# A Flamingo gated block on one core: the first steps behind the branch put in another order, and two filler products fewer

## The chip, the cores and the metric

The kernel runs on one core of one Trainium2 chip. The metric is the device time of one execution in microseconds (us); the figure for the kernel before is the median of three runs, 656.4 us (655.87 to 658.57).

## The reference

The inputs are `x` (16 sequences of 224 tokens, 512 wide), a context for each sequence (750 rows, 384 wide) and a mask of the context rows; which rows count is data, read on the chip. Cut to what matters:

```python
# x: (16, 224, 512)   context: (16, 750, 384)   mask: (16, 750)
q = (layernorm(x) @ W_q);  k = context @ W_k;  v = context @ W_v      # 8 heads of 64
sim  = where(mask, q k^T * 64**-0.5, -FMAX)
attn = softmax(sim) v
x = x + tanh(g_xattn) * (attn @ W_o + b_o)

def bitlinear(x, w, b):                    # int8-like rows, ternary weights
    xq = act_quant(rmsnorm(x));  wq = weight_quant(w)   # scale of w: mean(|w|) over all of w
    return xq @ wq.T + b
h = gelu(bitlinear(layernorm(x), w1, b1))  # 512 -> 2048
x = x + tanh(g_ffn) * bitlinear(h, w2, b2) # 2048 -> 512
```

## The kernel before

**Before the branch.** `order_batches` counts the mask rows, ranks the 16 sequences by how many context rows they need, and fetches the rows of the first place ("slot" 0) by gathers on POOL (GpSimd): two gathers of 128 tokens of `x` (`fetch_x`, L975) and two of context rows (`fetch_keys`, L1055). All engines then read one number, `n_odd`, and branch (L436, L437): if every slot fits its fixed capacity, the compact path runs, otherwise a dense one. The compact path runs here.

**Behind the branch.** The work is cut into named steps, and `ORDER`, a list written out by hand, gives the order in which they are issued. Each engine executes its own instructions in that order, and waits on semaphores for the others. So a place in the list is a place in the queue of every engine that the step uses. `s` counts slots (sequences in order of length), `t` blocks of 128 tokens, `i` pairs of such blocks. The steps that the change and the following sections speak of:

- `tokens` (L267 to L343, DVE): the table of row numbers for all later gathers of `x`: five small copies into `where`, and one multiply-add into `token`.
- `stats.0.k`, `rstd.0.k`, `norm.0.k`, k = 0 and 1 (L1258 to L1272): layernorm of the first two blocks of `x`. Mean and variance on DVE (`bs_x`, `mv_x`, `rs_x`), the power -1/2 on POOL (`rs_x<-rs_x,mhalf`, L1267), the normalising itself on DVE, in place (`xoT<-xoT,mv_x,rs_x`).
- `x.i.k` (L975, POOL): a gather of 128 rows of `x` by the table `token`; `ctx.s.t` (L1055, POOL): a gather of context rows by `keys`. POOL issues both, one after the other.
- `ind.s` (L1080, L1082, DVE, six instructions), `pi.s` (L1091, PE, two tiny products), `keys.s` (L1105, DVE, two instructions): the row numbers of the context rows that slot `s` keeps. `ind` has one buffer, so `ind.s` may begin only when the products of the slot before have read it.
- `warm` (L2137, PE): products of a matrix of ones with itself into a tile that nobody reads.
- `xnp.t` and `xnT.t.s`: turning the normalised rows on PE, and the copy out of PSUM; `ctxp`, `ctxT`: the same for context rows; `qp`, `kp`, `vp`, `vr`: the projections on PE; `sim`, `max`, `exp`: scores and softmax.
- `w.0.c` (L1992, SP's DMA queue): eight loads of 512 KB, the raw `w1`. `ws.0.c` sums their absolute values (DVE, L2006, where the list says `:v`; ACT, L2009, where it says `:s`); `wt.0` (L2019, DVE) adds the eight sums, `wtp.0` (L2024, PE) adds them across partitions, and `sw.0` gives the scale, without which no weight can be rounded. The same follows later for `w2` (`ws.1.c`, `wt.1`, `wtp.1`).
- `stats.i.k` for i > 0 (L1292, L1293, DVE): the statistics of a gathered block.

The buffers of PSUM that `pi`, `kp`, `qp` and others use come from one pool of four, given out in the order of the list; a step waits until the last reader of its buffer is done.

The selection steps in short:

```python
st["ind"] = ind = pa.tile([TJ, 192], BF16, tag="ind", bufs=1)            # ind.s
nc.vector.tensor_scalar(ind[:, at], place, sh.upto[:, 0, b : b + 1], None, ALU.is_ge)
for n in range(1, NJ):
    nc.vector.scalar_tensor_tensor(ind[:, at], place, sh.upto[:, n, b : b + 1], ind[:, at], ALU.is_ge, ALU.add)
```

Of the kernel before, what the change touches and what calls it, by code (L numbers as in the profile page):

```python
# [26 lines left out]
CAPS = (188, 188, 184, 180, 176, 168, 156, 148, 128, 124, 116, 104, 92, 80, 64, 64)  # L27

ORDER = """
hold.0 load.wv tokens stats.0.0 stats.0.1 rstd.0.0 rstd.0.1 x.2.0 norm.0.0 norm.0.1 ind.1 warm xnp.0 xnp.1 xnT.0.0:s  # L30
xnT.1.0:s xnT.1.1:s gap mask.0 ctxp.0.2 ctxp.0.0 qp.0.0 pi.1 ctxT.0.0:s ctxT.0.2:s keys.1 w.0.0 w.0.1 w.0.2 w.0.3
w.0.5 w.0.7 w.0.4 w.0.6 x.2.1 ctx.1.0 kp.0.0 ind.2 pi.2 x.1.0 x.1.1 ind.3 ws.0.1:s keys.2 stats.2.1 ctx.2.0 tanh
ws.0.0:v x.3.0 kp.0.2 kT.0.0:s stats.2.0 qT.0.0:s kT.0.0.c:s stats.1.1 rstd.2 ws.0.3:s sim.0.1 ws.0.2:v sim.0.0
ctx.1.1 kT.0.2:s ws.0.5:s vp.0 max.0.0.0 max.0.0.1 max.0.0.3 kT.0.2.c:s stats.1.0 exp.0.0.0 exp.0.0.1 max.0.1.0 rstd.1
exp.0.0.3 vr.0 max.0.0.2 v.0:s max.0.1.3 exp.0.0.2 norm.1.0 ws.0.4:v qp.0.2 v_rest.0:s norm.1.1 ws.0.7:s rec.0.0
# [888 lines left out]
def compact_path(ctx, tc, sh, x, context, out, late_rows, stages):  # L924
# [29 lines left out]
    def gen(shape, dtype, name):  # L954
        return ps_gen.tile(shape, dtype, tag="gen", name=name)
# [45 lines left out]
    def step(*key):  # L1001
        def keep(run):
            name = ".".join(str(k) for k in key)
            assert name not in steps, name
            steps[name] = run
            return run

        return keep
# [940 lines left out]
    @step("where")  # L1949
    def run():  # L1950
        late["where"] = [
            nc.values_load(
                sh.token[p : p + 1, t // 7, t % 7 : t % 7 + 1],
                engines=[mybir.EngineType.SP],
                min_val=0,
                max_val=B * S - n,
            )
            for p, t, n in ((0, NTOK - 4, 64), (64, NTOK - 4, S), (32, NTOK - 2, S))
        ]
# [115 lines left out]
    ctx = stages[0]  # L2075
# [57 lines left out]
    @step("warm")  # L2133
    def run():
        spare = gen([P, P], F32, "warm")
        for k in range(8):
            nc.tensor.matmul(spare, lhsT=sh.ones, rhs=sh.ones, start=True, stop=True)  # L2137

    @step("tokens")
# [76 lines left out]
```

## Time and profile before

| What | us |
|---|---|
| median of 3 runs (lowest, highest) | 656.4 (655.87, 658.57) |
| time of the profiled execution | 658.56 |
| its span | 656.8 |
| PE busy in the span | 633.6 (96%) |
| DVE, ACT, POOL busy | 494.2, 434.7, 380.8 |
| first product of the compact path that is read (`xnp.0`) | at 14.15 |
| longest waits of PE after that: for `wt.0`, then for `wt.1` | 2.7 (to 37.50), 1.8 (to 71.75) |

Times in the text are microseconds from the start of the span. Of the profiled execution's 658.56 us, 1.8 us lie outside the span. That execution was 2.2 us slower than the median. PE stands for TensorE's products and PEld for its weight loads, DVE for VectorE, ACT for ScalarE, POOL for GpSimd, SP for the engine that issues the plain DMAs. A wait is put down to the engine or transfer that ended it.

### The profile page before, as it was taken

The page shows a single profiled execution, that of the slowest core. Times are in us where ns is not written, and L with a number is a line of the kernel's source. Part 1 is how long each engine was busy: PE and PEld are TensorE (multiplying, and loading weights), DVE is VectorE, ACT ScalarE, POOL GpSimd, SP SyncE. Part 2 cuts the span into 40 slices and gives each one's busy share as a digit, 9 for nine tenths or more (in the row PEclk, how much of TensorE's full clock was granted, in tenths as well). Part 3 has the DMA queues.
Part 4 walks back from the last instruction along what each step waited for, and adds up shares of the span by engine and source line. Part 5 has one row for each costly group of instructions (what it writes and reads, how often), then busy time and mean ns, then how long its engine had stood idle before and what let it go on. Part 6 is the DMA issues. An engine that isn't in the chain of part 4 may idle for free.

```text
span 656.8 us, 11053 instructions
## 1 busy us (share of the span) xinstructions
PE 633.6 (96%) x3706; PEld 411.8 (63%) x3706; DVE 494.2 (75%) x1325; ACT 434.7 (66%) x985; POOL 380.8 (58%) x531
## 2 busy tenths in 40 slices
PE   6989899999999999999999999999999999999995
PEld 5767757767566585675756668656666755654442
DVE  6798788776874787777878577886595865858994
ACT  2489786767676673596757467875496554859694
POOL 6444558664866447663757763753776364564741
PEclk9999999999999999999999999999999999999999
DMA  6959682116233053312235521513243041433222
GB/s 204 371 81 304 196 199 69 45 49 110 66 87 86 32 80 91 84 34 61 65 77 80 96 75 34 92 46 58 64 117 73 17 97 50 95 65 81 48 33 86
DMA packets 97346, 60.73 MB, mean 92 GB/s; under 512 B 85461, under 2 KB 85609, under 8 KB 97152
## 3 DMA queue, kind: packets, MB, share of 16 engines
q1 hardware_dynamic: 89232, 35.41, 25.8%
q0 software_dynamic: 8048, 24.53, 12.4%
q8 instruction: 31, 0.51, 0.3%
q14 instruction: 35, 0.29, 0.1%
HBM read 31.87 MB, written 7.34 MB: 60 GB/s over the span
## 4 chain that ended last, share of the span: by engine, by line
PE 84%; DVE 6%; DMA 5%; ACT 2%; issue 1%; POOL 1%; DVEq 0%; POOLq 0%
PE hp L1671 14%; PE fp L1908 14%; PE qp L1345 14%; PE op L1547 13%; PE kp L1180 5%; PE vp L1207 5%; PE sim L1378 5%; PE ptp L1448 3%; PE av L1488 3%; DMA raw<-w 2%; PE xnp L1323 2%; DMA raw<-in_L_ffn_w_dram 2%; PE vr L1224 1%; DMA x<-in_x_dram,token 1%; PE ctxp L1160 1%
## 5 line engine op out<-in xcount | busy, mean ns | idle before, releaser
L1426 POOL TENSOR_TENSOR p<-p,rec 112x752 f32<-112x752 f32 (+13 forms) x64 | 73.2, 1149 | 134.4 <-DVE rec L1421 101.6
L1409 ACT ACTIVATE p<-p,nm 112x188 f32<-112x188 f32 (+13 forms) x256 | 102.0, 401 | 26.8 <-DVE nm L1395 25.8
L1345 PE MATMUL qp<-xnT,wq_sb 128*128 128x224 f32 x512 | 103.2, 355 | 0.0
L1671 PE MATMUL hp<-w1T,xqT 128*128 128x512 fp8e4 x448 | 102.1, 379 | 1.1 <-DVE h L1682 0.7
L1908 PE MATMUL fp<-w2T,hqT 128*128 128x512 fp8e4 x448 | 100.9, 379 | 0.7 <-ACT hqT L1713 0.7
L1547 PE MATMUL op<-wo_sb,xoT 128*128 128x512 f32 x224 | 101.0, 596 | 0.0
L1345 PEld LDWEIGHTS qp<-xnT,wq_sb 128*128 128x128 f32 x512 | 95.4, 190 | 4.9 <-issue 2.9
L1682 DVE SCALAR_TENSOR_TENSOR h<-hp,c,b_bc 128x1024 f32<-128x1024 f32 x52 | 66.6, 1282 | 31.3 <-PE hp L1671 26.5
L1671 PEld LDWEIGHTS <-xqT 128*128 128x128 bf16 x448 | 43.5, 98 | 51.3 <-issue 3.4
L1908 PEld LDWEIGHTS <-hqT 128*128 128x128 bf16 x448 | 43.1, 98 | 49.9 <-issue 1.1
L1547 PEld LDWEIGHTS op<-wo_sb,xoT 128*128 128x128 f32 x224 | 41.0, 190 | 44.7 <-issue 43.5
L1395 DVE CUSTOM_DVE_ANT_0 p<-sim,mask 112x64 f32<-112x64 f32 (+12 forms) x224 | 54.9, 281 | 18.7 <-PE sim L1378 12.0
L1731 DVE TENSOR_REDUCE a<-h 128x1 f32<-128x2048 f32 x26 | 59.2, 2277 | 1.1 <-ACT h L1726 1.1
L1726 ACT ACTIVATE h<-h 128x2048 f32<-128x2048 f32 x26 | 49.7, 1913 | 11.6 <-DVE h L1682 11.4
L1180 PE MATMUL kp<-ctxT,wk_sb 128*128 128x188 f32 (+12 forms) x360 | 52.4, 295 | 0.9 <-ACT pT L1025 0.9
L1180 PEld LDWEIGHTS kp<-ctxT,wk_sb 128*128 128x128 f32 x360 | 49.2, 191 | 5.9 <-issue 3.3
L1025 ACT COPY pT<-ptp 128x448 f32<-128x448 f32 (+6 forms) x54 | 28.1, 528 | 32.1 <-PE ptp L1448 30.1
L1409 ACT ACTIVATION_READ_ACCUMULATOR p<-p,nm 112x1 f32 x256 | 48.7, 190 | 0.0
L1757 ACT ACTIVATE h<-h 128x2048 f32<-128x2048 f32 x25 | 47.8, 1911 | 1.0 <-DVE hq L1737 1.0
L1378 PE MATMUL sim<-kT,qT 64*112 64x188 f32 (+13 forms) x512 | 42.5, 296 | 0.9 <-ACT xoT L1025 0.6
L1646 POOL TENSOR_TENSOR y<-y,b_bc 128x512 f32<-128x512 f32 x28 | 36.1, 1295 | 12.1 <-DVE xoT L1023 9.4
L1207 PE MATMUL vp<-wv_sb,ctxT 128*128 128x512 f32 (+5 forms) x90 | 41.6, 598 | 0.0
(211 smaller groups left out, 1161.4 us busy)
## 6 DMA issues: line engine op xcount, KB each, us to landing
raw<-in_L_ffn_w_dram SPq DMA_DIRECT2D x16, 512.0 KB, 5.5
wq_sb<-in_L_xattn_W_q_dram SPq DMA_DIRECT2D x1, 1024.0 KB
b_bc<-in_L_ffn_b_dram SPq DMA_DIRECT2D x1, 1024.0 KB
wk_sb<-in_L_xattn_W_k_dram SPq DMA_DIRECT2D x1, 768.0 KB
wv_sb<-in_L_xattn_W_v_dram SPq DMA_DIRECT2D x1, 768.0 KB
wo_sb<-in_L_xattn_W_o_dram SPq DMA_DIRECT2D x1, 512.0 KB, 11.6
wo_sb<-in_L_xattn_W_o_dram SPq DMA_DIRECT2D x2, 256.0 KB
out_dram<-y SPq DMA_DIRECT2D x2, 256.0 KB
```

The costliest lines, as they stand in the source:

```text
L1180: nc.tensor.matmul(pk[:, p - p0, :], lhsT=sh.wk[:, c, p * P : (p + 1) * P], rhs=st["ctxT"][:, c, :n], start=(c == 0), stop=(c == NC - 1),)
L1207: nc.tensor.matmul(pv[:w], lhsT=st["ctxT"][:, c, :w], rhs=sh.wv[:, c, :], start=(c == 0), stop=(c == NC - 1))
L1345: nc.tensor.matmul(pq[:, i, :], lhsT=sh.wq[:, d, (p + i) * P : (p + i + 1) * P], rhs=st["xnT"][:, d, :], start=(d == 0), stop=(d == ND - 1),)
L1378: nc.tensor.matmul(sim[:, j, i, :cap], lhsT=st["qT"][j * DH : (j + 1) * DH, p, q * TQ : (q + 1) * TQ], rhs=keys["kT"][j * DH : (j + 1) * D ...
L1395: nc.vector.tensor_tensor_reduce(out=probs[:, h, :cap], in0=box["sim"][:, j, i, :cap], in1=keys["mask"][:, first + j * begin : first + j * ...
L1409: nc.scalar.activation(box["p"][:, h, :cap], box["p"][:, h, :cap], AF.Exp, bias=box["nm", h], scale=-1.0, accum_out=total[:TQ, h : h + 1],)
L1426: nc.gpsimd.tensor_tensor(probs[:, :, first : first + cap], probs[:, :, :cap], box["rec"][:TQ].unsqueeze(2).to_broadcast([TQ, 4, cap]), AL ...
L1547: nc.tensor.matmul(po, lhsT=xoT[:, d, at : at + P], rhs=sh.wo[:, d, :], start=(d == 0), stop=(d == ND - 1))
L1671: nc.tensor.matmul(ph[:, n, :], lhsT=f["xqT"][:, k * ND + d, :], rhs=w1T[:, d, at : at + NB], start=(d == 0), stop=(d == ND - 1),)
L1682: nc.vector.scalar_tensor_tensor(h[:, cols], f["hp", k, g].rearrange("t i n -> t (i n)"), f["c1", k], sh.b1[:, cols], ALU.mult, ALU.add,)
L1731: nc.vector.tensor_reduce(amax[:, part], f["h", k], AX.X, ALU.max, apply_absolute_value=True)
L1908: nc.tensor.matmul(po, lhsT=f["hqT", k][:, n, :], rhs=w2T[:, n, :], start=(n == 0), stop=(n == NF - 1))
```

## The change

Three edits. In `ORDER`, `tokens` goes from ahead of the statistics of the first two blocks to behind their normalising, and `x.2.0` stays behind it. In `ORDER` again, `ind.2` goes from behind `kp.0.0` to ahead of `keys.1`. In `warm`, six products are issued in place of eight. Everything from `pi.2` on stands as it did.

```diff
 ORDER = """
-hold.0 load.wv tokens stats.0.0 stats.0.1 rstd.0.0 rstd.0.1 x.2.0 norm.0.0 norm.0.1 ind.1 warm xnp.0 xnp.1 xnT.0.0:s
-xnT.1.0:s xnT.1.1:s gap mask.0 ctxp.0.2 ctxp.0.0 qp.0.0 pi.1 ctxT.0.0:s ctxT.0.2:s keys.1 w.0.0 w.0.1 w.0.2 w.0.3
-w.0.5 w.0.7 w.0.4 w.0.6 x.2.1 ctx.1.0 kp.0.0 ind.2 pi.2 x.1.0 x.1.1 ind.3 ws.0.1:s keys.2 stats.2.1 ctx.2.0 tanh
+hold.0 load.wv stats.0.0 stats.0.1 rstd.0.0 rstd.0.1 norm.0.0 norm.0.1 tokens x.2.0 ind.1 warm xnp.0 xnp.1 xnT.0.0:s
+xnT.1.0:s xnT.1.1:s gap mask.0 ctxp.0.2 ctxp.0.0 qp.0.0 pi.1 ctxT.0.0:s ctxT.0.2:s ind.2 keys.1 w.0.0 w.0.1 w.0.2
+w.0.3 w.0.5 w.0.7 w.0.4 w.0.6 x.2.1 ctx.1.0 kp.0.0 pi.2 x.1.0 x.1.1 ind.3 ws.0.1:s keys.2 stats.2.1 ctx.2.0 tanh
 ws.0.0:v x.3.0 kp.0.2 kT.0.0:s stats.2.0 qT.0.0:s kT.0.0.c:s stats.1.1 rstd.2 ws.0.3:s sim.0.1 ws.0.2:v sim.0.0
...
     @step("warm")
     def run():
         spare = gen([P, P], F32, "warm")
-        for k in range(8):
+        for k in range(6):
             nc.tensor.matmul(spare, lhsT=sh.ones, rhs=sh.ones, start=True, stop=True)
```

On DVE the order of instructions becomes: `bs_x`, `mv_x`, `rs_x` twice, both normalisings, the six of `tokens`, `ind.1`, the fills and masks that stood behind it, `ind.2`, `keys.1`, `ind.3`, `keys.2`. On POOL nothing changes place: the two powers, then `x.2.0`, `x.2.1`, `ctx.1.0`, `x.1.0`, `x.1.1`, `ctx.2.0`. On PE the order is the same, with four instructions fewer (an f32 product is two). ACT and SP are as before.

## The prediction

> **What bounds the kernel now.** I read the page's busy shares and its chain first.
>
> ```profile
> PE 633.6 (96%) x3706; PEld 411.8 (63%) x3706; DVE 494.2 (75%) x1325; ACT 434.7 (66%) x985; POOL 380.8 (58%) x531
> PE 84%; DVE 6%; DMA 5%; ACT 2%; issue 1%; POOL 1%; DVEq 0%; POOLq 0%
> ```
>
> PE is the bound, and between 100 and 600 us it hardly ever stands still (over 99.8% busy in those windows). The change leaves all of that work alone. What it can move is the time at which PE's unbroken run begins, so the chain in order of time is read next, over the first 38 us (start, length, what).
>
> ```profile
> 11.44 0.19 DVE token L343
> 11.63 0.61 DVE bs_x L1258
> ...
> 23.72 6.31 DMA x<-in_x_dram,token
> 30.05 0.70 DVE bs_x L1292
> ...
> 37.50 0.37 PE wtotp L2024 x2
> ```
>
> The table `tokens` stands in the chain ahead of the first statistics; the selection of slot 1 leads to POOL's gathers; the gather of `x.1.1` takes 6.31 us from issue to use and ends a wait of DVE, whose next instructions then run without a gap until `wt.0`. PE waits for that sum; this is its longest wait behind the branch (time, count, longest):
>
> ```profile
> PE wtotp L2024 <- DVE wtot L2019: 4.5, 2, 2.7
> DVE bs_x L1292 <- DMA x<-in_x_dram,token: 0.7, 1, 0.7
> DVE keys L1105 <- PE pi L1091: 2.4, 1, 2.4
> ```
>
> After 37.50 PE runs full until 60, and the rounding of the weights hangs on the same sum, through their transposes and the loads of `w2` to the second such wait at 71.75. So a shift of `stats.1.1` at 30.05 goes through to the end, one for one. That is the quantity to work out.
>
> **Edit one, statistics ahead of the table.** `tokens` occupies DVE from 10.36 to 11.63, 1.27 us. Without it the first statistics start at 10.36: their data came from a gather issued at 5.87, and the context gather issued at 9.38 released ACT at 12.49, 3.11 later, so I put the two blocks at 9.0 and 10.5 at the latest, both in time. `rs_x` is then ready at 11.4 in place of 12.63. But POOL stands ahead of the gain:
>
> ```profile
> 11.70 0.50 POOL L222 IOTA place_f<- 128x192 bf16 x2
> 12.15 0.10 POOL L337 MEMSET mhalf<- 128x2 f32 x1
> 12.79 0.59 POOL L1267 TENSOR_TENSOR rs_x<-rs_x,mhalf 128x1 f32<-128x1 f32 x1 [0.54 <-DVE rs_x L1262]
> 13.72 0.78 POOL L1267 TENSOR_TENSOR rs_x<-rs_x,mhalf 128x1 f32<-128x1 f32 x1 [0.35 <-DVE rs_x L1262]
> ```
>
> POOL issues gathers until 11.65 and fills `mhalf` until 12.25. The first power can come no earlier than 12.3: 0.5 gained of 1.27. The second follows at 12.9 and, at its slower 0.78, ends at 13.7 in place of 14.50; the second normalising ends 0.8 earlier. On PE `xnp.0` moves from 14.15 to 13.66 and `xnp.1` from 15.19 to 14.5, since its four products ahead (0.85) now set it: 0.7 for everything up to `qp.0.0` and `pi.1`. The instructions that move back: `tokens` now runs from about 14.3 to 15.6, and `ind.1`, the fills and masks end at 18.7 in place of 18.22. The 2.4 us in which DVE waited for `pi.1` hide that. On POOL `x.2.0` must now wait for `token` and goes from 14.68 to 15.7; only `x.2.1` and `ctx.1.0` queue behind it, and POOL was idle for 4.0 us ahead of `ctx.1.0`. The rows of `x.2.1` are wanted at 26.51; with 6.31 from an issue at 17.0 they land at 23.3. Cost: nothing, unless landing took over 9 us.
>
> **Edit two, `ind.2` ahead of `keys.1`.**
>
> ```profile
> 20.62 0.33 DVE L1105 TENSOR_SCALAR keys<-pi,first 128x1 int32<-128x1 f32 x2 [2.40 <-PE pi L1091]
> 20.88 0.25 DVE L1080 TENSOR_SCALAR ind<-place,upto 125x192 bf16<-125x192 bf16 x1
> 21.11 1.00 POOL L1055 DMA_INDIRECT ctx<-in_ctx_dram,keys  x1 [4.01 <-DVE keys L1105]
> 21.17 2.24 DVE L1082 SCALAR_TENSOR_TENSOR ind<-place,upto,ind 125x192 bf16<-125x192 bf16 x5
> ```
>
> `ind.2` takes 20.88 to 23.41, 2.53 us, and may not start before `pi.1` has read the buffer, so it inherits the wait of `keys.1`. `keys.1` then comes 2.53 later against `pi.1`. Queued behind its wait on POOL: `ctx.1.0`, `x.1.0` and `x.1.1`, all late by 2.53, 1.3 us apart. In return `pi.2`, `ind.3`, `keys.2` come some 0.3 earlier against `pi.1`, being spared the 0.33 of `keys.1` or part of it. `kp.0.2` takes the PSUM buffer of `pi.1` and now waits for `keys.1`; that ends about when it used to start (23.69 before, 3.2 us behind `pi.1` in both orders): nothing.
>
> **Edit three, six products.** Eight took 10.14 to 13.89, 0.47 us each. PE then waited 0.26 for the normalising. Two fewer end at 12.95, so `xnp.0` at 13.66 isn't blocked; eight would cost it 0.23. But these products also keep PE active, and its pace is seen to change (min/median/max ns of one turning product):
>
> ```profile
> L1323 PE MATMUL xnp<-ident,xoT x8: 397/421/477, 14.2 to 15.9; 128*128 128x128 f32 x8
> L1323 PE MATMUL xnp<-ident,x x8: 272/273/331, 38.3 to 41.3; 128*128 128x128 f32 x8
> ```
>
> The same product took 421 early and 272 late, 298 on average in `ctxp` from 16.10, though the clock column says 1.00 for both. PE comes to full pace near 16.1, after some 5.6 us of products. If the same sum is needed, full pace comes 0.3 later (0.94 less work, 0.5 earlier start, most of it in `ctxp`): I take +0.3. The bounds: nothing, or all of `qp.0.0` (3.22) at the early pace, another 2.9.
> [...]
>
> **The sum.** `pi.1` releases DVE at 20.62 - 0.7 + 0.3 = 20.2. `x.1.1` is issued at 23.72 - 0.4 + 2.53 = 25.85. DVE reaches `stats.1.1` at 29.35 - 0.4 - 0.2 = 28.75, so its landing decides. Rows: 6.31 while the weights load, 3.11 when little else does. The transfer share by window says which is nearer (us, PE, PEld, DVE, ACT, POOL busy, clock, DMA share, GB/s):
>
> ```profile
> 26.00:32.00 6.00, 6.00 (x37) 3.38 (x36) 5.19 (x12) 2.38 (x6) 4.13 (x6) 1.00 1.03 380
> 32.00:40.00 8.00, 5.27 (x39) 4.55 (x39) 7.46 (x30) 6.91 (x27) 4.78 (x7) 1.00 0.07 18
> ```
>
> The queues are full to about 32. The gathers' bytes only move later, so the weights clear a little sooner; I take 6.0. Landing 31.85 against 30.05: **+1.8 us**. DVE's wait there grows from 0.7 to about 3, PE's wait for `wt.0` from 2.7 to about 5. Against the profiled execution: 658.56 + 1.8 = 660.4. That execution lay 2.2 above the median; the same shift on the median gives 656.4 + 1.8 = **658.2**, which is 0.3% and inside the 0.5% (3.3 us) that a measurement of this kernel can tell from no change.
> [...]
>
> **The rivals.**
> *The gathers are not late where it counts.* If landing is set by the end of the weight loads and not by the issue, `x.1.1` lands 3.11 after its issue, at 28.96: 1.1 earlier than before, 655.3; the floor is DVE's own 28.75, -1.3. For it: the gathers no longer compete from 25 on. Against it: 380 GB/s until 32, and all eight loads are issued before 20.
> *PE's clock, slower by over 0.5%.* One mechanism: too little activity. All of `qp.0.0` at the early pace gives 2.6 more than my 0.3, so +4.4, 660.8; the growth of PE's wait for `wt.0` from 2.7 to 5 can do it a second time, as the products behind 37.5 would run at 421 in place of 272 (2.7 us of idle left them at 272). It decides from 1.5 us on top of my sum. Against it: half of what PE loses behind 37.5 comes back in its waits of 0.9 and 1.8 us before 71.75.
> *Edit one brings nothing* (POOL no earlier than 12.79): `pi.1` 0.7 later, +2.5, 658.9; within the forecast's range.
>
> **How the numbers follow.** Forecast with its variants, +0.2 to +3.2: 0.58, own range 656.6 to 659.6. Clock, over +3.3: 0.30, plus 0.02 for landings slower than 6.31. Gathers in time, -1.3 to 0, with the scatter of single runs (655.87 to 658.57) about it: 0.10, of which 0.04 over 0.5% faster. Slower 0.32, faster 0.04, the same 0.64. The range leaves out one in ten on each side: 655.4 from the second case, 661.2 from the clock at +4.4 with a little scatter.
>
> **What would show it.** Right: first power on POOL near 12.3, `keys.1` about 2.2 later than 20.62, DVE waiting 2 to 4 us for `x` at L1292, PE's wait for `wt.0` near 5, and no other stage changed in length. Wrong: no wait at L1292 (the landing), `pi.1` at 21 or later with `qp` products over 400 ns (the clock), or a shift at 37.5 that is gone by 72.

## The result and the profile after

The changed kernel takes 660.1 us (median of 10 runs, 658.41 to 660.95) against 656.3 us of the kernel before (10 runs beside it, 655.73 to 658.57). The ratio is 1.0047, 95% interval 1.0037 to 1.0058: slower by 3.1 us (2.4 to 3.8). The forecast was 658.2 with a range of 655.4 to 661.2; the time lies inside the range, between the forecast's own upper end (659.6) and the clock rival (660.8). Ratios here and below leave out single executions more than 1.5% above the fastest of their kernel (five in all, at 740 to 3708 us).

The page of the changed kernel, its busy shares and its chain:

```profile
PE 634.6 (97%) x3702; PEld 412.4 (63%) x3702; DVE 494.0 (75%) x1325; ACT 434.5 (66%) x985; POOL 379.7 (58%) x531
PE 87%; DVE 4%; DMA 3%; ACT 2%; issue 2%; POOL 1%; DVEq 0%; POOLq 0%; ACTq 0%
```

PE was busy for 1 us longer with four instructions fewer: some products ran more slowly (in the timelines the sixteen of `sim` near 40 take 2.94 in place of 1.58). The chain in order of time shows which (start, length, what):

```profile
12.45 0.60 POOL rs_x L1267
...
13.67 1.27 PE xnp L1323 x8
14.95 0.94 PE ctxp L1160 x6
15.89 3.23 PE qp L1345 x16
...
21.82 0.26 DVE keys L1105 x2
...
24.82 6.16 DMA x<-in_x_dram,token
31.00 0.70 DVE bs_x L1292
...
38.46 0.56 PE wtotp L2024 x2
39.02 0.93 PE ctxp L1160 x4
39.95 1.04 PE xnp L1323 x4
41.00 0.51 PE ctxp L1160 x2
41.50 2.59 PE sim L1378 x16
```

The first power starts at 12.45 (12.79 before). `qp.0.0` ends and `pi.1` starts at 19.12, 1.3 earlier than before. `keys.1` then stands behind `ind.2` and comes at 21.82, 1.2 later than before, and `x.1.1` is issued 1.1 later. It lands at 31.00, and everything behind it follows. In the list of waits (total, times, longest) DVE's wait for it has grown from 0.7 to 3.2 and PE's for the sum of the weights from 2.7 to 5.3:

```profile
PE wtotp L2024 <- DVE wtot L2019: 5.3, 1, 5.3
DVE bs_x L1292 <- DMA x<-in_x_dram,token: 3.2, 1, 3.2
```

Behind that wait PE's clock falls to half. Stretches of the changed kernel (us, busy time of PE, PEld, DVE, ACT, POOL, then the granted clock, DMA share, GB/s):

```profile
36.00:37.50 1.50, 0.00 (x0) 0.00 (x0) 1.50 (x5) 1.45 (x6) 1.48 (x2) 1.00 0.04 11
37.50:41.00 3.50, 2.54 (x11) 1.93 (x11) 2.78 (x10) 1.83 (x8) 2.20 (x3) 0.51 0.00 0
41.00:44.30 3.30, 3.30 (x20) 2.71 (x20) 3.27 (x8) 2.17 (x9) 0.00 (x0) 0.50 0.53 104
44.50:48.00 3.50, 3.50 (x26) 3.50 (x25) 3.43 (x9) 1.90 (x5) 0.00 (x0) 1.00 0.93 153
```

From about 37.5 to 44.3, 6.8 us, PE ran at half clock. The same two stretches of the kernel before:

```profile
37.50:41.00 3.50, 3.50 (x33) 2.87 (x34) 3.07 (x10) 2.88 (x12) 1.27 (x2) 1.00 0.00 0
41.00:44.30 3.30, 3.30 (x24) 3.30 (x23) 3.29 (x7) 2.02 (x7) 0.00 (x0) 1.00 1.48 160
```

The second sum of the weights reached PE at 73.20 (71.75 before).

**Two profiled executions are a bad pair here.** Their spans, 656.8 and 657.1, differ by 0.3, the medians by 3.8. The last addition to `y` shows where the rest is hidden. Before:

```profile
650.01 0.75 DVE y L1931
```

After:

```profile
651.69 0.75 DVE y L1931
```

At that point the changed kernel is 1.7 late. What follows is only the last write of the output, and it took 6.0 us to the end of the span before (656.8 - 650.76) and 4.7 after. The kernel before had also met PE's clock later at its start (`xnp` 2.13 us long, 1.27 after). So differences of single profiles are read below only between executions whose `xnp.0` and `xnp.1` took about as long.

### The profile page after: what moved, and what is told of

Read it like the earlier page. It is cut to its first block, busy times and chain, and to the rows that moved or that the text cites. A ratio compares the mean times of both kernels' runs of the same rounds, so it can differ in the third digit from the quotient of the medians.

```text
span 657.1 us, 11046 instructions
## 1 busy us (share of the span) xinstructions
PE 634.6 (97%) x3702; PEld 412.4 (63%) x3702; DVE 494.0 (75%) x1325; ACT 434.5 (66%) x985; POOL 379.7 (58%) x531
## 4 chain that ended last, share of the span: by engine, by line
PE 87%; DVE 4%; DMA 3%; ACT 2%; issue 2%; POOL 1%; DVEq 0%; POOLq 0%; ACTq 0%
PE qp L1345 15%; PE hp L1671 14%; PE fp L1908 14%; PE op L1547 13%; PE kp L1180 6%; PE vp L1207 6%; PE sim L1378 5%; PE ptp L1448 4%; PE av L1488 3%; PE xnp L1323 2%; PE vr L1224 2%; DMA raw<-w 1%; PE ctxp L1160 1%; PE av L1502 1%; PE ptr L1462 1%
## 5 line engine op out<-in xcount | busy, mean ns | idle before, releaser
L1025 ACT COPY pT<-ptp 128x448 f32<-128x448 f32 (+6 forms) x54 | 28.1, 528 | 33.7 <-PE ptp L1448 31.7
L1378 PE MATMUL sim<-kT,qT 64*112 64x188 f32 (+13 forms) x512 | 43.9, 303 | 1.2 <-ACT xoT L1025 0.7
```

The source lines that it names most:

```text
L1378: nc.tensor.matmul(sim[:, j, i, :cap], lhsT=st["qT"][j * DH : (j + 1) * DH, p, q * TQ : (q + 1) * TQ], rhs=keys["kT"][j * DH : (j + 1) * D ...
```

## The experiments

My theory after the result: edit one gains, edit two delays the gather of `x.1.1`, and the longer wait of PE costs its clock as well. The rivals: the six products (edit three) or the earlier statistics do it; or the shift is all and the clock costs nothing. Each kernel was timed beside the kernel before, so all ratios are to that (0.001 is 0.66 us).

**1. Edits one and three without edit two.**

```diff
-... ctxT.0.2:s ind.2 keys.1 ... kp.0.0 pi.2 x.1.0 x.1.1 ind.3
+... ctxT.0.2:s keys.1 ... kp.0.0 ind.2 pi.2 x.1.0 x.1.1 ind.3
```

> Edits one and three alone: ind.2 is back behind kp.0.0. Theory (edit two alone costs, by the late gather of x.1.1): pi.1 near 19.0 as after the change, keys.1 near 19.3, x.1.1 issued near 22.3 and landed by 28.6, DVE hardly waits at L1292, PE's wait for wt.0 near 2.9 and the sum at 36.1 in place of 37.5 before; no stretch at half clock behind it; 655.2, from 654.9 to 655.8, 0.5 to 1.4 below the kernel before. Rival (the six products or the earlier statistics take PE's clock away): wait of 5 or half clock behind 38 still there, 658.5 or more.

Measured: 656.74, ratio 0.9998 (0.9984 to 1.0012). Without edit two the loss is gone, but so is the expected gain. Ten of the 12 runs lie at 655.3 to 657.5, two at 660.1 and 661.2, and the profiled one is the slowest. Its chain:

```profile
13.67 1.97 PE xnp L1323 x8
15.64 1.53 PE ctxp L1160 x6
17.17 5.95 PE qp L1345 x16
23.12 0.14 PE pi L1091 x2
```

Every row is the same work, started at the same 13.67 as in the changed kernel, and lasts 1.6 to 1.8 times as long: in this execution PE came to full pace only near the end of `qp.0.0`, and `pi.1` came 4.0 later. That is the first half of the clock rival, seen in one execution; the other run over 660 was not profiled. This profile also has the half clock that I had ruled out here, from 39.7 to 46.6 (`sim` 2.59 long at 42.91), behind a wait of only 2.4 for the sum. So a wait of 5 is not needed for it.

**2. Edit two alone.**

```diff
-... ctxT.0.2:s keys.1 ... kp.0.0 ind.2 pi.2
+... ctxT.0.2:s ind.2 keys.1 ... kp.0.0 pi.2
```

> The kernel before with ind.2 ahead of keys.1 and nothing else. Theory: keys.1 at 23.1, x.1.1 issued near 25.9 and landed near 32, DVE waits about 2 at L1292, the sum for PE comes 1.5 to 2 later than 37.50, PE waits 4 to 5 us for it; with that wait its clock falls to half for one or two windows of 3.4 us: 659.5 to 662, 3 to 5.5 above the kernel before. Shift without clock: 658.2. Rival (edits one or three to blame): within 0.7 of the kernel before, 656 to 657.

Measured: 659.74, ratio 1.0039 (1.0027 to 1.0052). Both waits are there:

```profile
PE wtotp L2024 <- DVE wtot L2019: 5.1, 1, 5.1
DVE bs_x L1292 <- DMA x<-in_x_dram,token: 3.0, 1, 3.0
```

`wtotp` came at 39.25, and behind it `sim` was 2.59 long as in the changed kernel. Edit two alone is enough.

**3. The changed kernel with eight products.**

```diff
-        for k in range(6):
+        for k in range(8):
```

> The changed kernel with eight early products again. Theory: the products have nothing to do with the loss; xnp.0 starts up to 0.23 later, the wait for wt.0 stays at 5 and the half clock behind it too: 659.4 to 660.9, within 0.7 of the changed kernel (660.1). Rival (six products too few to hold the clock): no stretch at half clock and 656 to 658.

Measured: 659.43, ratio 1.0038 (1.0026 to 1.0050); `wtotp` at 38.45, half clock from 37.5 to 44.3 again. The six products are not what takes the clock there. The mean granted clock of every run is on record, and it says that this is no matter of the profiled ones alone: it is 0.991 to 0.994 in all 27 runs of the changed kernel and of experiments 2 and 3, and 0.995 to 0.999 in the ten shorter runs of experiment 1. (6.8 us at half clock take 0.005 off the mean; PE's idle end of the span, also at half clock, took at most 0.003 in these profiles.) What eight save in the changed kernel, 0.0009, is inside the intervals.

**4. Edit one alone** (the changed kernel with eight products and `ind.2` in its old place).

> Edit one alone: statistics ahead of the table, eight early products, ind.2 in its old place. Theory: with eight products PE is at full pace by 17 in every run; pi.1 near 19.2 in place of 20.6, x.1.1 issued near 22.4 and landed by 28.8, DVE hardly waits at L1292, the sum of wt.0 reaches PE near 36.2 in place of 37.50, PE's wait for it 2.7 to 3.0, no half clock behind it: 655.3, from 654.7 to 655.9, and none of the runs at 660 that edits one and three together showed in 2 of 12. Rival (six products are harmless, those two runs were chance): as edits one and three together, 656.7 with runs at 660. Rival (landing is set by the weight loads): no gain, 656.5 to 657.

Measured: 656.09, ratio 0.9986 (0.9975 to 0.9998): a gain of 0.9 us (0.1 to 1.6), at a median just above the range that I had given. Nine of the 12 runs lie at 655.1 to 656.4, but three are at 657.6 to 659.3, so eight products do not remove the scatter as I expected. The profiled one, the slowest, shows a possible cause that I had not expected:

```profile
37.50:41.00 3.50, 3.50 (x35) 3.00 (x35) 3.33 (x9) 2.98 (x11) 0.72 (x1) 1.00 0.04 8
73.40:76.70 3.30, 3.30 (x11) 2.85 (x9) 2.93 (x5) 2.15 (x10) 0.00 (x0) 0.50 0.17 56
```

The clock survived the wait of 3.0 for the first sum, and was lost at 73.4, behind a wait of only 1.7 for the second.

**5. Edit three alone** (the kernel before with six products).

> The kernel before with six early products in place of eight. [...] The working in the prediction (0.3 at most from the missing work): 656.7 to 657.3 with the scatter of the kernel before. Rival (clock not touched): within 0.3 of the kernel before.

Measured: 659.57, ratio 1.0032 (1.0016 to 1.0049), single runs from 656.06 to 660.22. Removing two products whose result nobody reads costs 2.1 us (1.1 to 3.2) in the old order. In the profiled execution (657.57, one of the faster) PE's groups between 10 and 24 us show the gap (busy, mean ns of one, idle before):

```profile
L1345 PE MATMUL qp<-xnT,wq_sb 128*128 128x224 f32 x16 | 4.9, 480 | 0.0
L2137 PE MATMUL warm<-ones 128*128 128x128 f32 x12 | 2.9, 432 | 0.5 <-DVE keys L1049 0.5
...
L1323 PE MATMUL xnp<-ident,xoT 128*128 128x128 f32 x8 | 1.3, 286 | 1.5 <-DVE xoT L1272 1.5
```

PE stood for 1.5 us ahead of the eight `xnp`, in two waits of which the longer took 1.1. The clock was full there, and fell back to half for the stretch behind; it did so again behind the wait of 2.6 for the first sum:

```profile
13.00:16.60 3.60, 2.09 (x14) 1.33 (x13) 2.98 (x9) 1.21 (x3) 2.78 (x4) 1.00 0.56 191
16.80:20.00 3.20, 3.20 (x10) 2.86 (x9) 1.47 (x7) 0.70 (x2) 0.39 (x1) 0.50 1.04 381
40.60:44.00 3.40, 3.40 (x22) 2.95 (x19) 3.37 (x7) 2.01 (x9) 0.00 (x0) 0.50 0.43 83
```

`qp.0.0` took 4.80 in place of 3.22. How the runs near 660 looked was not profiled. Their mean granted clock of 0.998 to 1.000 (seven runs from 659.1 up) leaves no room for such a fall: it alone would take off 0.0026. A late start like that of experiment 1 would not show in this figure, since the column reads 1.00 ahead of the first grant (1.00 from 10 to 14 us in the kernel before, where the first grant came at 16.13), so it is the likelier cause; it is not shown.

**6. The gathers that need only the table go first** (the changed kernel with eight products).

```diff
-... x.2.1 ctx.1.0 kp.0.0 pi.2 x.1.0 x.1.1 ind.3
+... x.2.1 x.1.1 x.1.0 ctx.1.0 kp.0.0 pi.2 ind.3
```

> The changed kernel with eight early products and with the gathers x.1.1 and x.1.0, which need only the table, issued ahead of ctx.1.0 instead of behind it: they no longer wait for keys.1. Theory: x.1.1 is issued near 18.5 and landed by 26, DVE does not wait at L1292 and reaches stats.1.1 at 27.8, the sum of wt.0 reaches PE near 35.3 (38.45 with the late gather, 37.50 before), PE's wait for it is about 2, no half clock behind it: 655.0, from 654.3 to 655.8, 4.4 below the changed kernel with eight products. Rival (the sums wait for the weights, which land at 32 whatever the gathers do): PE's sum at 37 or later, 656 to 657. Rival (the gather does not matter, only ind.2 ahead of keys.1 does): 659.4.

Measured: 655.93, ratio 0.9984 (0.9973 to 0.9995), against 1.0038 for the same kernel with the gathers behind `keys.1`. So `ind.2` ahead of `keys.1` costs, as far as can be told, only by way of these gathers; what they alone would gain in the old order was not run. The waits between 18 and 40 us:

```profile
PE wtotp L2024 <- DVE wtot L2019: 3.4, 1, 3.4
...
DVE wsums L2006 <- DMA raw<-in_L_ffn_w_dram: 1.3, 1, 1.3
```

The wait for `x` is gone, and the next one stands in its place: DVE now waits for the weights themselves. The sum reached PE at 36.54, not at 35.3. The first rival's mechanism was right for 1.2 of the 3.1 us that I had hoped for. And the half clock that I had ruled out is there, from 37.5 to 40.9, behind a wait of 3.4.

**7. The same with six products** (the changed kernel with that one move).

> The changed kernel, six early products, with one move: x.1.1 and x.1.0 issued ahead of ctx.1.0. Against the same with eight products (655.9) it shows what edit three costs where edit one has shortened its gap to 0.7. Theory: in some runs full clock comes one or two windows later (20 to 23 us), and everything with it; median 656.2 to 657.2, with single runs of 658.5 to 660. Rival (six are as good as eight here): 655.9, no run over 657.2.

Measured: 655.70, ratio 0.9989 (0.9973 to 1.0005); 11 runs from 654.5 to 657.6 and one at 660.5. Against eight products the difference is 0.0005, unclear: the median fits the rival, and the stray run, as in experiment 1, the theory. Its profiled execution again shows the clock (stretches ahead of, behind and after the first sum):

```profile
33.20:36.80 3.60, 0.91 (x7) 0.70 (x8) 3.16 (x11) 2.68 (x11) 3.09 (x4) 1.00 0.02 6
36.90:40.20 3.30, 3.30 (x20) 2.97 (x21) 3.23 (x6) 2.58 (x10) 0.00 (x0) 0.50 0.14 28
40.30:44.00 3.70, 3.70 (x29) 3.46 (x27) 3.67 (x10) 1.51 (x4) 0.00 (x0) 1.00 0.97 181
```

A wait of 2.8 cost one stretch of 3.4 us at half clock.

**8 to 10. What the clock costs: products in the gaps.** The late gather stays, and PE is kept busy while it waits. Experiment 8 fills the first gap of the changed kernel, 9 does so with eight early products, 10 fills the second gap too.

```diff
-            box["pt"] = pt = gen([P, 1], F32, f"wtotp_{wi}")
+            box["pt"] = full = gen([P, P], F32, f"wtotp_{wi}")
+            for k in range((18, 7)[wi]):
+                nc.tensor.matmul(full, lhsT=sh.ones, rhs=sh.ones, start=True, stop=True)
+            box["pt"] = pt = full[:, 0:1]
```

(18 and 0 in experiments 8 and 9.)

> The changed kernel with 18 products of ones ahead of the product of wt.0, in the gap in which PE waits for that sum; their result is overwritten. The gather is as late as in the changed kernel, DVE's wait of 3.2 stays and the sum comes at 38.3 to 38.7. Theory (half of the loss is PE's clock, which falls in the empty gap): granted clock back at 0.998, xnp behind the sum at 272 ns, sum behind it 1.6 long and not 2.6; 657.0 to 658.2, some 2 to 3 below the changed kernel and 0.7 to 1.8 above the kernel before. Rival (the loss is all the late gather): as the changed kernel, 659.5 to 661.

> The changed kernel with eight early products and 18 products of ones ahead of the product of wt.0, their result overwritten: the late gather without half clock behind it, against the changed kernel with eight products (659.4). The sum of wt.0 reaches PE near 38.5 in both. Theory now: the way through the weights to the second such sum takes 34.0 from the first (34.25 in the kernel before, 33.8 with 18 products and six), so full clock can bring that sum from 73.2 to no earlier than 72.4: 658.4 to 659.2, a gain of 0.3 to 1.0. Rival (half of the loss is clock): 656.9 to 657.9. Rival (clock costs nothing): 659.4.

Measured: 659.48, ratio 1.0031 (1.0020 to 1.0042), and 660.00, ratio 1.0040 (1.0023 to 1.0056). Without fillers the two kernels stood at 1.0047 and 1.0038: the gain of experiment 8, 0.0016, is at the edge of what the intervals can tell, and experiment 9 gains nothing. The clock behind the first sum was full in both (`sim` 1.31 long at 40.95 in experiment 9, 2.59 in the changed kernel). My 657 to 658 for experiment 8 was wrong. Its profile lost the clock later, from 74.2 to 77.6, behind a wait of 1.7 for the second sum. In experiment 9 PE, ahead of time again, waited 1.6 for the second sum and lost its clock there:

```profile
73.00:78.00 5.00, 5.00 (x18) 4.45 (x18) 4.11 (x11) 3.38 (x14) 1.67 (x2) 0.66 0.28 74
```

The ten runs of experiment 9 fall into two groups: five with a mean granted clock of 0.999 or 1.000 took 657.6 to 659.5, five with 0.995 to 0.997, the profiled one among them, took 660.5 to 661.6. The 2.8 us between the medians of the groups is more than the 1.7 that I estimate for 3.4 us at half clock (half of them), so something else differs between them too, and what it is was not looked for.

> The changed kernel with eight early products, and with products of ones in both gaps in which PE waits for a sum of the weights: 18 ahead of the first and 7 ahead of the second (result overwritten). With 18 and none, half clock only moved from 38 to 74 us, and the runs that had it nowhere lay near 658.4. Theory (a late sum costs 2 and the clock that PE loses while it waits costs about 1 more): no half clock between the start and 650 in any run, second sum near 72.6, 658.0, from 657.4 to 658.7. Rival (the clock costs nothing, the runs near 658.4 were chance): 659.4 to 660, as with fillers in the first gap alone.

Measured: ratio 1.0028 (1.0018 to 1.0039), median 658.87, and the same stretch at full clock:

```profile
73.00:78.00 5.00, 5.00 (x36) 4.35 (x36) 4.22 (x11) 3.93 (x16) 1.20 (x2) 1.00 0.24 76
```

It is between theory and rival. The fillers of the second gap were a little too many: they, and not the sum, came last there (`71.39 1.76 PE wtotp` in the chain, the product itself at 73.15).

**11. Fillers on edit one alone** (experiment 4 with 12 and 7 such products).

> Edit one alone with eight early products, and 12 and 7 products of ones in the two gaps ahead of the sums of the weights (3.0 and 1.75 us there; result overwritten). Theory: the runs with a granted clock of 0.994 (657.6 and more with edit one alone) are those that lost it in a gap; they go, the others stay: 655.4, from 654.9 to 656.0, none over 657. Rival (their scatter comes from the start or from transfers): 656.1 with runs at 657.6 and more.

Measured: 656.77, ratio 0.9993 (0.9983 to 1.0004); 656.0 to 658.2. The theory missed: the clock was full in the profile, but the shortest runs of experiment 4 (655.1 to 655.7) went with the longest. Here too the fillers of the second gap came last: they ended at 70.60, DVE's sum at 70.10. Between 10 and 11, both with full clock, edit two makes 0.0035, 2.3 us; between 3 and 4, without fillers, 0.0052, 3.4 us. The difference, 1.1, is the estimate for the clock; the intervals of the four ratios are each about 0.7 us to either side, so it is not settled that it differs from zero. The direct differences, 1.1 from the changed kernel to experiment 8 and 0.7 from 3 to 10, are of the same size and as uncertain.

**12. Early gathers, eight products and fillers** (experiment 6 with 13 and 5).

> The changed kernel with eight early products, x.1.1 and x.1.0 issued ahead of ctx.1.0, and 13 and 5 products of ones in the two gaps (result overwritten). Theory: first sum near 36.5 as without fillers, no half clock behind it, second sum near 70.5, 1.2 earlier than in the kernel before (71.75): 654.6, from 653.9 to 655.4, the fastest of these kernels. Rival (the way through the weights sets the end, so that full clock buys nothing): 655.9 as without fillers.

Measured: 656.48, ratio 0.9986 (0.9976 to 0.9997), not the 654.6 of the theory. With experiments 4 and 6 it is one of three kernels that beat both kernels, by about 1 us; the fillers add nothing that can be measured. Its chain says why:

```profile
36.05 0.29 PE wtotp L2027 x2
...
51.47 4.96 DMA raw<-w
...
57.53 10.61 DMA raw<-in_L_ffn_w_dram
68.16 1.23 DVE wsums L2006
69.70 0.38 PE wtotp L2027 x2
```

With PE at full clock the second sum hangs on the weights' transposes and loads, as in the kernel before: 33.65 us from sum to sum.

## Why the prediction was right or wrong

**Edit one** was forecast at 0.5 at the first power and 0.7 at `pi.1`. The power came 0.34 earlier. `pi.1` came 1.3 earlier in the profile, but 0.86 of that is PE's pace in `xnp` (2.13 long before, 1.27 after), which differs from execution to execution (1.97 for the same rows in experiment 1). By itself the edit gains 0.9 us (0.1 to 1.6). The step stands, and that `tokens` and `x.2.0` could move back at no cost stands too: DVE's one wait for `x` in the changed kernel is that for `x.1.1`.

**Edit two** is the mechanism that was forecast, and its size was right. At like paces of the start (`xnp` 1.71 and 1.60 long) the profile of experiment 9 against that of 4 gives 2.7 later at `keys.1` and at the issue of `x.1.1` (25.62 against 22.96), 2.2 at the landing (31.75 against 29.52) and 2.1 at the first sum (39.12 against 36.98). Experiment 4:

```profile
22.96 6.53 DMA x<-in_x_dram,token
36.98 0.37 PE wtotp L2024 x2
```

Experiment 9:

```profile
25.62 6.11 DMA x<-in_x_dram,token
39.12 0.38 PE wtotp L2027 x2
```

I had 2.53 for the instructions of `ind.2`, and 2.2 at the landing once edit one's share is taken off (1.8 + 0.4). The landing took 6.16 (6.0 taken, 3.1 to 6.3 as bounds). DVE's wait was to be about 3 and is 3.2, PE's about 5 and is 5.3.

**"One for one" to the second sum** holds to about half a microsecond where PE keeps its clock or loses one stretch of it: the way from sum to sum took 34.25 before and 33.7 to 34.3 in eight of the nine experiments that lost at most 3.4 us of clock behind the first sum (34.9 in experiment 4). In the changed kernel and experiments 1, 2 and 3, with 6.8 us at half clock, it took 34.7 to 35.1, and PE itself, no longer the weights, came last at 73. That is the point named against the clock rival, that PE's waits of 0.9 and 1.8 ahead of 71.75 give back half: they shrank to 0.4 and 0.2 in the changed kernel, which gave back 2.1, and then were used up.

**The clock behind 37.5** is the step that failed. I let PE's wait grow from 2.7 to 5 and kept the products behind it at full pace in the forecast, with 0.30 for the clock. I had taken one execution, in which 2.7 us of idle left the products at full pace, as a sign that such gaps do no harm; experiment 5 lost the clock behind 2.6. The chance was too low: every kernel with the wait of 5 and no fillers lost the clock in its profile, and by the mean granted clock (0.991 to 0.994) in every run. In time it is worth about 1.1 us, and by the intervals that could be nothing or 2.5.

**Edit three** was put at +0.3, with bounds of 0 and 2.9, next to edit one. Alone, in the old order, for which the prediction has no term, it costs 2.1 (1.1 to 3.2). The gap that it opens there is 1.5 in the profile; that this gap is the cause in the slower runs is not shown. Next to edit one the gap is only 0.5 in the profile of the changed kernel, and the differences of three pairs of kernels, eight products against six, are 0.0012 (4 and 1), 0.0009 (3 and the changed kernel) and 0.0005 (6 and 7): 0.3 to 0.8 us each, none clear by itself, all of one sign. So the 0.3 is not refuted. The single runs hint at a rare loss of about 4 rather than a shift of all: of 24 runs with six products next to edit one and no long wait (experiments 1 and 7) three are over 660, of 24 with eight (4 and 6) none. The variants of the forecast reach +3.2, 1.4 above its sum, which leaves room for a larger loss by edit three; no run shows one of that size as a shift of the whole kernel next to edit one: the pairs give 0.3 to 0.8, the single runs about 4.

**The sum.** Edit one -0.9 (experiment 4), edit two +3.4 (from 4 to 3), edit three +0.6 (from 3 to the changed kernel): 3.1. It closes because the three are steps along one line. What is independent is that edit two alone makes 2.6 (1.8 to 3.4) from the other side. Against my 1.8 the excess is the clock behind the first sum (about 1.1) and edit three (0.6 in place of 0.3); neither is clear of zero by itself, so this division is an estimate. The range held because it had been drawn to reach the clock rival: the forecast's own sum, without that loss, is 1.3 short.

**The rivals.** The gathers in time: refuted by the wait of 3.2. That the weights end the wait was seen only when the gathers had been moved ahead. Edit one brings nothing: refuted, narrowly. Clock: seen in both of its places, at less than its price (a late start in the slowest run of experiment 1, the fall behind 37.5 in all profiles with the long wait and no fillers).

## What to carry to other kernels

A reordering that only moves a small transfer later must be followed to the wait that it ends, and then to what the longer wait does to the engine behind it: on PE, a gap of 2.6 us was followed by 3.4 us at half clock in experiment 5, and one of 2.7 by none in the kernel before. Products that nobody reads may be holding the clock (two of them fewer cost 2.1 us in experiment 5, and its profile has half clock from 16.8 to 20.0 behind 1.5 of idle); count the idle time that their removal opens, not the time that it saves. Where the moved work shares a queue with transfers that don't need it (here the gathers of `x`, which need only the table), put those first; here the place of `ind.2` could then no longer be seen in the time (0.9984 in experiment 6, 0.9986 in experiment 4).

## What the hardware showed that I had not expected

Gaps no longer than the half-clock stretch, and some of half its length, were followed by one: idle times of PE ahead of a sum of 1.6 (experiment 9), 1.7 (4 and 8), 2.6 (5), 2.8 (7) and 3.4 us (6) were each followed by about 3.4 us at half clock, and one of 2.4 (1) by 6.8, while 3.0 us in experiment 4 and 2.7 in the kernel before were not. Gaps of nearly the same length (2.6 in experiment 5, 2.7 in the kernel before) were thus followed by a loss in one execution and by none in another.

A good part of the chance is where the gap falls. In the fourteen profiles each of the eleven falls of the clock between its first grant and 80 us comes a whole number of steps of 3.41 us after that grant (in the changed kernel 37.56 - 13.67 = 23.89, seven steps). Laid out in such steps, each with at least 2.3 us of idle PE (six of them) was followed by half clock, and none with at most 1.2 was; of the seven with 1.35 to 1.84, five were. So the gap of 3.0 in experiment 4, cut in two by the end of a step, cost nothing, and the gap of 1.7 within one step did (PE's busy time is the second figure behind the stretch):

```profile
32.36:35.77 3.41, 1.67 (x9) 1.32 (x7) 3.38 (x13) 3.35 (x13) 2.31 (x5) 1.00 0.06 18
35.77:39.18 3.41, 2.21 (x20) 1.83 (x22) 2.90 (x10) 2.74 (x13) 2.45 (x3) 1.00 0.00 0
69.90:73.32 3.42, 1.67 (x16) 1.49 (x10) 2.63 (x9) 3.42 (x10) 2.08 (x3) 1.00 0.43 147
```

A wait of over 5 us, however it falls, leaves more than 2.5 us of idle in one such step (an estimate from the 3.41); the changed kernel, with its wait of 5.3, lost its clock in its profile, and its mean granted clock is 0.991 to 0.994 in all ten runs. What decides between 1.35 and 1.84 is not shown: the first and the third row have the same busy time.

Keeping the clock up at the one place moved the loss to the next: with fillers in the first gap PE arrived early at the second sum, waited 1.6 and lost the clock there (1.7 in experiment 8). And with full clock from 13 to 650 us (experiment 11; mean granted clock 0.998, the idle end included) the kernel was not faster than with the scatter (0.9993 against 0.9986), though its fillers may have held the second sum for up to 0.5 us (70.10 to 70.60, above).

The last write of the output took 4.7 to 6.0 us from the same instruction in the two profiles shown, for reasons that I did not look for. That alone is over a third of the effect that was to be measured.
